# Silu made from tanh, and a causal mask added in tiles of 32 rows

## The chip, the core and the metric

The kernel runs on one core of a Trainium2 chip. The core has engines that run side by side, each through its own instructions in order: TensorE (PE: matrix products, with the weight loads shown apart as PEld), VectorE (DVE), ScalarE (ACT), GpSimd (POOL) and SyncE (SP, which here only starts transfers). They wait for each other through semaphores. PE writes to PSUM, of which this kernel uses eight banks of 128 x 512 floats. Transfers run in queues on 16 DMA engines. The metric is the device time of one execution in microseconds (us).

## The reference

The input `x` is 16 sequences of 256 rows with 128 columns. Four blocks are added to it, each after a layer normalization:

```python
x = x + attention_a(layernorm(x))      # 2 heads of 64, rotary half, softmax, full
x = x + ffn(layernorm(x))
x = x + attention_b(layernorm(x))      # 16 heads of 8, causal (see below)
x = x + ffn(layernorm(x))              # the same weights again
```

The feed-forward block has ternary weights `w` and a scale `s` for each output:

```python
h = silu(x @ w1.T * s1) * (x @ w2.T * s2)     # 128 -> 512
h = gelu(h @ h1.T * t1); h = gelu(h @ h2.T * t2)   # 512 -> 512, exact gelu
return h @ w3.T * s3                           # 512 -> 128
```

In attention b the scores are `k . q / sqrt(8)`, replaced by -10000 wherever the key's row is later than the query's, and the softmax runs over the keys.

## The kernel before, in words

**Tiles.** The 4096 rows are eight tiles (`NP`) of 512 rows, two sequences each. All of `x` stays on chip in `XR`. Each tile goes through attention a, feed-forward "f", attention b and feed-forward "g". Attention b works by sequence: for each, four groups of four heads.

**Order.** The loops at the end of `hybrid_kernel` record every operation, with the engine, an expected time and a rank, in a `Plan`. `Plan.laid` then places them in time like a list scheduler: at each step it takes, over all engines, the operation that can begin first; among those of one engine whose start is within a small margin (line 230) the one with the lowest rank wins, and `ORDER` (line 341) gives ranks by stage and tile. The planner knows that ACT needs `LOAD` more when the table of functions has to change (`mode`), and that PE loses `SWITCH` when it goes between matmuls on all 128 rows ("1"), on row tiles ("2r", "4r") and on column tiles ("2c", "4c"). Some operations are recorded with two or three engines (`either`), and the planner picks. `Plan.emit` writes the result out, so all instructions have line 291 in the profile, and groups are told apart by tile names.

**PSUM.** Four banks together are one tile `s` (`g_scores`, one slot): a group of scores fills it, and the next must wait until it is read. The other four banks are the tiles `w` (`g_bank`); every other product passes through them.

**Feed-forward** (`ffn`). For each of four parts of 128 hidden units, PE makes `pu` and `pg` in two banks. ACT computes Silu of `pu` into `u`; DVE multiplies `pg`, its scale and `u`, the gate product. Then `u` is split (`parts`) into a rounded high part and the rest, each 128 x 512, because the products with the hidden weights `h_sb` are exact only as a sum of both parts. ACT, DVE or POOL rounds; DVE or POOL subtracts. The hidden layers read all four parts; ACT computes Gelu from the bank. Three tables of ACT matter: Silu's, Gelu's and the exponential's, which both attentions need.

**Attention b.** The queries and keys of a tile are written to DRAM by SP (`far_q`, `far_k`) and read back by POOL's queue in another layout (`qk`). In the maxima step (`attention_b_max`) PE makes a group of scores with eight matmuls of 32 rows in "4r" mode: four heads lie on four groups of 32 rows, write to four banks, and run side by side. The mask is then added in the same banks by four matmuls of full height, one for each head:

```python
for a in range(4):
    o.matmul(sc[:, a, P : 3 * P], lhsT=eye[:], rhs=hide[:], start=False, stop=True, ...)
```

`eye` is the identity and `hide` a 128 x 256 table with -3e38 where a score must not count (the diagonal block, twice). DVE reduces the group to maxima, 1.75 us. Later `attention_b` makes the scores again ("4r", tiles `s`, with the maxima through `pick`), ACT takes the exponential (1.45 us), POOL cuts the upper triangle off, and PE multiplies by the values in "4c" mode.

**Set-up.** Constants are made on POOL and DVE (rank `LATER`) while the loads run. Columns of scales lie in `cols_sb`: `C_W1S` holds `s1`, `C_W2S` holds `s2`.

Of the kernel before, what the change touches and what calls it, by code (L numbers as in the profile page):

```python
# [94 lines left out]
class Plan:  # L95
# [2 lines left out]
    HOP = {"PE": 0.26, "DVE": 0.12, "ACT": 0.14, "POOL": 0.1, "SP": 0.1}  # L98
    LOAD = 1.28
    SWITCH = 0.17  # L100
    WEIGH = {"ACT": 1.54, "PE": 0.00}
    BRANCH = 1.6

    def __init__(self, nc):
# [64 lines left out]
    def laid(self):  # L169
# [28 lines left out]
        for _ in range(len(self.ops)):  # L198
            best = None
            for e, ops in ready.items():  # L200
                cands = []
                for op in ops:
                    at = max(op.at, free[e])
                    wants = {}
                    for t in op.main.tiles | op.main.claims:
                        g = t.group
                        if t.slot is None and g is not None:
                            n = wants[g] = wants.get(g, 0) + 1
                            at = max(at, sorted(g.free)[n - 1], min(t.quota.free) if t.quota else 0.0)
                    for g, n in wants.items():  # L210
                        if g.in_turn and not all(t in op.main.tiles | op.main.claims for t in g.queue[:n]):
                            at = 1e9
                    if at >= 1e8:
                        continue
                    if cut is not None and e not in behind and at >= cut:
                        at = max(at, cut + self.BRANCH)
                    cost = 0.0
                    if op.mode is not None and op.mode != mode[e]:
                        if e == "ACT" and not (isinstance(op.mode, tuple) and mode[e] in op.mode):
                            cost = self.LOAD  # L220
                        elif e == "PE" and (op.mode[0] if isinstance(op.mode, tuple) else op.mode) != mode[e]:
                            cost = self.SWITCH
                    cands.append((at, cost, op))
                if not cands:
                    continue

                weigh = self.WEIGH.get(e, 0.0)
                first = min(a + weigh * c for a, c, _ in cands)
                at, cost, op = min(
                    (x for x in cands if x[0] + weigh * x[1] <= first + 0.012),  # L230
                    key=lambda x: (order_of(x[2].main.rank), x[2].main.index),
                )
                if best is None or (at, at + cost + op.us) < (best[0], best[0] + best[1] + best[2].us):
                    best = (at, cost, op)
# [59 lines left out]
class _Recorder:  # L294
# [19 lines left out]
P = 128  # L314
# [24 lines left out]


ORDER = {
    (INPUT, "a"): (-781, 18.6),
    (MAIN, "a"): (-863, 52.3),
    (NORM, "f"): (377, 0),
    (FILL, "f"): (88, 87.2),
    (INPUT, "b"): (299, 73.8),
    (MAXIMA, "b"): (-1830, 180.0),
    (MAIN, "b"): (448, 22.6),
    (NORM, "g"): (827, 180.7),
    (FILL, "g"): (423, 113.4),  # L350
}
LATER_AT = -505


def order_of(kind):
# [20 lines left out]
def hybrid_kernel(ctx: ExitStack, tc: tile.TileContext, x, rows, cols, wa, wb, w12, h1, h2, w3, out):  # L376
# [127 lines left out]
    for t in range(2):  # L504
# [11 lines left out]
    o.tensor_scalar(rot2[:, :, 1, :], ya[:], -1.0, None, ALU.mult)  # L516
    o.tensor_scalar(rot1[:, :, 1, :], rot2[:, :, 0, :], -1.0, None, ALU.mult)


    p.rank = (LATER, "", 0, 0)  # L520
    ones = fixed([P, P], "ones")
# [2 lines left out]
    p("POOL", 0.1).memset(neg[:], NEG)  # L524


    hide = fixed([P, 2 * P], "hide", BF16)
    o = p("POOL", 0.8)
    o.memset(hide[:], 0.0)
    o.affine_select(  # L530
        out=hide[:].rearrange("p (b k) -> p b k", b=2),
        in_=hide[:].rearrange("p (b k) -> p b k", b=2),
        compare_op=ALU.is_ge,
        fill=-HUGE,
        base=0,
        pattern=[[0, 2], [-1, P]],
        channel_multiplier=1,
    )
    eye = fixed([P, P], "eye", BF16)
    p("POOL", 0.3).tensor_copy(eye[:], ident[:])  # L540

    least = fixed([P, 2], "least")
    o = p("POOL", 0.5)
# [36 lines left out]
    o.tensor_scalar(pi[:], pi[:], 31, 1, ALU.bitwise_and, ALU.arith_shift_right)  # L580
    o.tensor_tensor(pick4[:], pi[:], want[:], ALU.is_equal)
    p("DVE", 0.46).tensor_copy(pick[:], pick4[:].unsqueeze(2).to_broadcast([P, 4, P]))

    s8 = 1.0 / math.sqrt(DB)
    p("POOL", 0.3).tensor_scalar(wb_sb[:, 0:P], wb_sb[:, 0:P], s8, None, ALU.mult)
# [46 lines left out]
    def bank(name, quota=None):  # L632
        return p.tile(psum, [P, 512], F32, name, g_bank, quota)

    def sb(shape, name, g, quota=None, dtype=F32):
        return p.tile(work, shape, dtype, name, g, quota)

    def small(shape, name):

        n = math.prod(shape[1:])  # L640
# [7 lines left out]
    def layernorm_T(i, what, bias=None):  # L648
# [20 lines left out]
        for t in range(TB):  # L669
            by, mean = rstd[:, t : t + 1], mv[:, t, 0:1]  # L670
            p.either(
                ("DVE", 0.26, "tensor_scalar", (xh[:, t, :], XR[i][:, t, :], mean, by, ALU.subtract, ALU.mult), {}),
                ("ACT", 0.24, "activation", (xh[:, t, :], XR[i][:, t, :], AF.Identity), {"bias": shift[:, t : t + 1], "scale": by}),
            )
        pt = bank(f"lt_{what}{i}", ahead)
        parts = what in "fg"
# [127 lines left out]
    def attention_b_inputs(i):  # L804
# [3 lines left out]
        for name, c0, bias in (("q", 0, C_BQ), ("k", P, C_BK)):  # L808
            plus = cols_sb[:, bias : bias + 1]
            pp = bank(f"p{name}b{i}", ahead)  # L810
            hl = sb([P, 2, TOK], f"{name}hl{i}", g_16, q_hl, F32R)
            p("PE", 0.45, "1", claim=[hl]).matmul(pp[:], lhsT=wb_sb[:, c0 : c0 + P], rhs=xT[:], start=True, stop=True)
            p.either(
                ("ACT", 0.67, "activation", (hl[:, 0, :], pp[:], AF.Identity), {"bias": plus}),
                ("DVE", 0.72, "tensor_scalar", (hl[:, 0, :], pp[:], plus, None, ALU.add), {}),
            )
            p("DVE", 0.77).scalar_tensor_tensor(hl[:, 1, :], pp[:], plus, hl[:, 0, :], ALU.add, ALU.subtract)
# [24 lines left out]
    def attention_b_max(i, s, q0, k0, q1, k1, v):  # L842
# [10 lines left out]
        for g in range(4):  # L853


            sc = p.tile(psum, [P, 4, 512], F32, f"sb{n}_{g}", g_scores)
            o = p("PE", 0.28 + 0.15 + 0.42, ("4r", "1"))
            for qt, c0 in ((1, 0), (0, T)):
                for a in range(4):
                    rows = slice(32 * a, 32 * a + 32)  # L860
# [192 lines left out]
    def ffn(i, what):  # L1053
# [23 lines left out]
        for o in range(NC):  # L1077
# [11 lines left out]
        for layer, (w_sb, wv, cs) in enumerate(((h1_sb, h1v, C_H1S), (h2_sb, h2v, C_H2S))):  # L1089
# [110 lines left out]
```

## Time and profile before

| | |
|---|---|
| runs of the kernel | 787.37 us median of 3 (785.58 to 787.78) |
| profiled execution | 785.15 us; its span, first to last instruction, 783.4 us |
| busy: PE, ACT, DVE, POOL | 718.8, 529.7, 499.7, 269.5 us |
| table loads on ACT | 103, 1283 ns each |
| mask matmuls | 256 of 128 x 256 |
| Silu; gate product | 64 on ACT, 688 ns; 64 on DVE, 744 ns |
| granted PE clock, mean | 0.984 |

In the page, each engine's busy time is followed by its share of the span; the slices cut the span in 40, and a digit is the busy share in tenths. The chain goes back from the last instruction, at each step to what released it or to the instruction before it on its engine; its shares tell where the end was set. A row of a group reads: engine, operation, output tile <- input tiles, shape, count | busy us, mean ns of one | idle time ahead of them and what ended most of it. A row of waits reads: who <- for whom: us in total, times, longest. A row of a timeline reads: start, duration in us, engine, what. The end of a matmul is modelled, so starts are the better measure on PE.

### The profile page before, as it was taken

What the parts mean: (1) busy time and instruction counts of PE and PEld (TensorE: products, weight loads), DVE (VectorE), ACT (ScalarE), POOL (GpSimd) and SP (SyncE); (2) the same over time, 40 slices, a digit from 0 to 9 for tenths busy, and PEclk for the clock granted to TensorE, in tenths of its full rate; (3) what the DMA queues carried; (4) which work ended last, traced back from release to release, by engine and by line L of the source; (5) the groups of instructions that cost most, each with busy time, mean ns of one, the idle gap of its engine ahead of it and who ended that gap; (6) DMA issues with size and microseconds to landing.
All of it is one profiled execution on the core that took longest, in us unless ns stands there. A gap on an engine that the chain in (4) does not pass through costs nothing.

```text
span 783.4 us, 14329 instructions
## 1 busy us (share of the span) xinstructions
PE 718.8 (92%) x5700; PEld 510.5 (65%) x5700; DVE 499.7 (64%) x1051; ACT 529.7 (68%) x790; POOL 269.5 (34%) x422
## 2 busy tenths in 40 slices
PE   4796899988999999999999999899998989999996
PEld 2564566767677775775675768576665765756775
DVE  6887896485864866656666674856666467463641
ACT  4566777774689759776657675765768566689652
POOL 8765554042406315144325422313324233131000
PEclk9798999999999999999999999999999999999999
DMA  8400000006004225043052110404322022000000
GB/s 295 143 1 1 1 1 1 1 25 191 1 33 129 54 109 162 1 133 84 2 161 54 33 24 1 123 1 121 97 79 56 1 69 55 2 14 2 14 15 18
DMA packets 37789, 45.20 MB, mean 58 GB/s; under 512 B 1744, under 2 KB 26832, under 8 KB 37712
## 3 DMA queue, kind: packets, MB, share of 16 engines
q0 software_dynamic: 18096, 19.40, 10.2%
q1 hardware_dynamic: 19328, 24.39, 8.9%
q8 instruction: 46, 0.75, 0.4%
q10 hardware_dynamic: 288, 0.39, 0.2%
q14 instruction: 31, 0.25, 0.1%
HBM read 25.31 MB, written 18.87 MB: 56 GB/s over the span
## 4 chain that ended last, share of the span: by engine, by line
PE 64%; DVE 16%; ACT 10%; issue 4%; POOL 3%; DMA 2%; SPq 0%; POOLq 0%; DVEq 0%; ACTq 0%
PE w L291 53%; PE s L291 11%; ACT L291 3%; ACT w L291 3%; DVE u L291 2%; DVE small L291 2%; DVE h L291 2%; DVE w L291 2%; DVE m L291 2%; ACT u L291 2%; POOL w L291 1%; DVE x L291 1%; DMA x<-in_x 1%; ACT hl L291 1%; POOL rope L291 1%
## 5 line engine op out<-in xcount | busy, mean ns | idle before, releaser
L291 PE MATMUL w<-h,h_sb 128*128 128x512 f32 x1024 | 278.2, 411 | 6.2 <-DVE h L291 1.9
L291 PEld LDWEIGHTS w<-h,h_sb 128*128 128x128 f32 x1024 | 182.2, 189 | 58.2 <-issue 5.4
L291 ACT ACTIVATE u<-w,cols_sb 128x512 f32<-128x512 f32 x128 | 87.3, 687 | 76.3 <-PE w L291 75.5
L291 ACT ACT_TABLE_LOAD x103 | 132.1, 1283 | 9.5 <-DVE small L291 4.8
L291 POOL TENSOR_SCALAR_AFFINE_SELECT w<-w 128x1024 f32<-128x1024 f32 x64 | 71.7, 1120 | 192.3 <-ACT w L291 187.8
L291 DVE TENSOR_REDUCE m<-s 128x12 f32<-128x1536 f32 x64 | 112.3, 1754 | 25.2 <-PE s L291 24.6
L291 ACT ACTIVATE w<-s 128x1536 f32<-128x1536 f32 x64 | 92.9, 1451 | 25.7 <-PE s L291 20.9
L291 DVE TENSOR_TENSOR h<-u,h 128x512 fp32r<-128x512 f32 x102 | 72.7, 713 | 31.0 <-ACT h L291 28.7
L291 PE MATMUL s<-qk,qk 32*128 32x256 f32 x1024 | 73.3, 331 | 7.3 <-ACT w L291 3.6
L291 PEld LDWEIGHTS s<-qk,qk 32*128 32x128 f32 x1024 | 44.5, 184 | 47.4 <-issue 15.1
L291 DVE SCALAR_TENSOR_TENSOR u<-w,cols_sb,u 128x512 f32<-128x512 f32 x64 | 47.6, 744 | 38.6 <-ACT u L291 38.6
L291 ACT ACTIVATE hl<-w,cols_sb 128x512 f32<-128x512 f32 x64 | 41.7, 687 | 37.7 <-PE w L291 37.5
L291 PE MATMUL w<-w_sb,hl 128*128 128x128 f32 x512 | 62.1, 276 | 0.5 <-ACT hl L291 0.3
L291 PE MATMUL w<-xTffn,w_sb 128*128 128x512 f32 x128 | 57.4, 448 | 4.2 <-ACT u L291 1.8
L291 PEld LDWEIGHTS w<-w_sb,hl 128*128 128x128 f32 x512 | 59.6, 192 | 2.1 <-ACT hl L291 1.2
L291 PE MATMUL w<-w,vp 128*32 128x256 f32 (+1 forms) x1024 | 54.3, 331 | 3.6 <-POOL w L291 2.5
L291 POOL TENSOR_TENSOR h<-u,h 128x512 fp32r<-128x512 f32 x26 | 33.4, 1289 | 63.0 <-ACT h L291 51.7
L291 PE MATMUL w<-xlffn,w_sb 128*128 128x512 f32 x128 | 52.8, 413 | 1.6 <-DVE xlffn L291 1.6
L291 DVE TENSOR_TENSOR x<-w,x 128x512 f32<-128x512 f32 (+1 forms) x40 | 23.1, 579 | 47.8 <-PE w L291 47.7
L291 PEld LDWEIGHTS w<-w,vp 128*32 128x32 f32 x1024 | 27.1, 109 | 31.4 <-issue 11.1
L291 ACT CAST h<-u 128x512 fp32r<-128x512 f32 x66 | 40.9, 620 | 4.3 <-DVE u L291 2.3
L291 ACT ACTIVATE w<-s,small 128x256 f32<-128x256 f32 x64 | 29.5, 478 | 16.1 <-DVE small L291 12.7
(156 smaller groups left out, 1080.5 us busy)
## 6 DMA issues: line engine op xcount, KB each, us to landing
far_q<-w SPq DMA_DIRECT2D x16, 512.0 KB, 3.0
far_k<-w SPq DMA_DIRECT2D x16, 512.0 KB, 3.7
qk<-far_q POOLq DMA_DIRECT2D x16, 512.0 KB, 4.3
qk<-far_k POOLq DMA_DIRECT2D x16, 512.0 KB, 5.0
w<-in_h SPq DMA_DIRECT2D x2, 1024.0 KB, 11.2
h_sb<-in_h POOLq DMA_DIRECT2D x2, 1024.0 KB, 10.6
out<-x SPq DMA_DIRECT2D x8, 256.0 KB, 2.4
x<-in_x SPq DMA_DIRECT2D x7, 256.0 KB, 9.2
```

Source lines behind the costliest of these rows:

```text
L291: getattr(getattr(self.nc, self.ENGINES[op.engine]), name)(*a, **k)
```

## The change

- In `ffn`, ACT computes `tanh(s1/2 * pu)` in place of Silu; the planner may run it under the exponential's table or under Gelu's. A new DVE product makes `(u + 1) * pu` in place. The set-up halves `C_W1S` and multiplies `C_W2S` by it (two POOL instructions), so that the gate product gives the same value.
- In `attention_b_max` the mask is added by sixteen matmuls of 32 rows in place of four of 128. For each slice of 32 rows of the mask there are four, one for each head's row group, and the slice leaves out the columns ahead of it, which hold nothing: they have 256, 192, 128 and 64 columns. `eye` and `hide` become tables of four slices, 128 x 512 each, built from two iotas on POOL and five DVE instructions. The step is now all "4r".
- Expected times, ranks (`ORDER`, `LATER_AT`), the weight of a table load (`WEIGH`) and the margin in the planner have other values, so the order on every engine and the choices among engines are different.

```diff
-    WEIGH = {"ACT": 1.54, "PE": 0.00}
+    WEIGH = {"ACT": 0.37, "PE": 0.00}
...
-                    (x for x in cands if x[0] + weigh * x[1] <= first + 0.012),
+                    (x for x in cands if x[0] + weigh * x[1] <= first + 0.010),
...
-    (INPUT, "a"): (-781, 18.6),
-    (MAIN, "a"): (-863, 52.3),
-    (NORM, "f"): (377, 0),
-    (FILL, "f"): (88, 87.2),
-    (INPUT, "b"): (299, 73.8),
-    (MAXIMA, "b"): (-1830, 180.0),
-    (MAIN, "b"): (448, 22.6),
-    (NORM, "g"): (827, 180.7),
-    (FILL, "g"): (423, 113.4),
+    (INPUT, "a"): (-887, 5.0),
+    (MAIN, "a"): (-1031, 75.9),
+    (NORM, "f"): (333, 26.5),
+    (FILL, "f"): (-481, 27.8),
+    (INPUT, "b"): (371, 24.9),
+    (MAXIMA, "b"): (-1664, 7.9),
+    (MAIN, "b"): (-33, 10.3),
+    (NORM, "g"): (1277, 199.8),
+    (FILL, "g"): (-595, 156.8),
 }
-LATER_AT = -505
+LATER_AT = -277
...
+    skew = sb([P, 4, P], "skew", g_16, None, I32)
+    p("POOL", 0.7).iota(skew[:], pattern=[[-32, 4], [1, P]], base=0, channel_multiplier=0)
+    rowi = fixed([P, 1], "rowi", I32)
+    p("POOL", 0.1).iota(rowi[:], pattern=[[0, 1]], base=0, channel_multiplier=1)
+    row = fixed([P, 1], "row")
+    away = sb([P, 4, P], "away", g_16)
+    o = p("DVE", 0.7)
+    o.tensor_scalar(rowi[:], rowi[:], 31, None, ALU.bitwise_and)
+    o.tensor_copy(row[:], rowi[:])
+    o.tensor_copy(away[:], skew[:])
+    eye = fixed([P, 4, P], "eye", BF16)
+    hide = fixed([P, 4, P], "hide", BF16)
+    o = p("DVE", 0.7)
+    o.tensor_scalar(eye[:], away[:], row[:, 0:1], None, ALU.is_equal)
+    o.tensor_scalar(hide[:], away[:], row[:, 0:1], -HUGE, ALU.is_gt, ALU.mult)
...
+    p("POOL", 0.2).tensor_scalar(cols_sb[:, C_W1S : C_W1S + NC], cols_sb[:, C_W1S : C_W1S + NC], 0.5, None, ALU.mult)
+    p("POOL", 0.2).tensor_tensor(
+        cols_sb[:, C_W2S : C_W2S + NC], cols_sb[:, C_W2S : C_W2S + NC], cols_sb[:, C_W1S : C_W1S + NC], ALU.mult
+    )
...
-                ("ACT", 0.24, "activation", (xh[:, t, :], XR[i][:, t, :], AF.Identity), {"bias": shift[:, t : t + 1], "scale": by}),
+                ("ACT", 0.38, "activation", (xh[:, t, :], XR[i][:, t, :], AF.Identity), {"bias": shift[:, t : t + 1], "scale": by}),
...
-            o = p("PE", 0.28 + 0.15 + 0.42, ("4r", "1"))
+            o = p("PE", 0.55, "4r")
...
-            for a in range(4):
-                o.matmul(sc[:, a, P : 3 * P], lhsT=eye[:], rhs=hide[:], start=False, stop=True, skip_group_check=True)
+            for sl in range(4):
+                for a in range(4):
+                    rows = slice(32 * a, 32 * a + 32)
+                    o.matmul(
+                        sc[:, a, P : 3 * P].rearrange("p (b k) -> p b k", b=2)[:, :, 32 * sl : P],
+                        lhsT=eye[rows, sl, :],
+                        rhs=hide[rows, sl, 32 * sl : P].unsqueeze(1).to_broadcast([32, 2, P - 32 * sl]),
+                        start=False,
+                        stop=sl == 3,
+                        skip_group_check=True,
+                    )
...
-            p("ACT", 0.59, "silu", rank=(FIRST, what, i, 0)).activation(u[:], pu[:], AF.Silu, scale=cols_sb[:, C_W1S + o : C_W1S + o + 1])
+
+            p("ACT", 0.59, ("exp", "gelu"), rank=(FIRST, what, i, 0)).activation(
+                u[:], pu[:], AF.Tanh, scale=cols_sb[:, C_W1S + o : C_W1S + o + 1]
+            )
+            p("DVE", 0.77, rank=(FIRST, what, i, 0)).scalar_tensor_tensor(u[:], u[:], 1.0, pu[:], ALU.add, ALU.mult)
...
-                p("ACT", 0.59, "gelu", rank=(FIRST, what, i, 0)).activation(u, ph[:], AF.Gelu, scale=cols_sb[:, cs + o : cs + o + 1])
+                p("ACT", 0.65, "gelu", rank=(FIRST, what, i, 0)).activation(u, ph[:], AF.Gelu, scale=cols_sb[:, cs + o : cs + o + 1])
```

The expected times of the bias additions of attention b's inputs change too (ACT 0.67 to 0.59, DVE 0.72 to 0.66 and 0.77 to 0.67).

More of the change, by code (lines that the diff above doesn't have):

```diff
@@ L517, in hybrid_kernel, with sb @@
     o.tensor_scalar(rot1[:, :, 1, :], rot2[:, :, 0, :], -1.0, None, ALU.mult)
+    def sb(shape, name, g, quota=None, dtype=F32):
+        return p.tile(work, shape, dtype, name, g, quota)
     p.rank = (LATER, "", 0, 0)
@@ L524, in hybrid_kernel @@
     p("POOL", 0.1).memset(neg[:], NEG)
[L527 to L540, printed above, removed]
+    skew = sb([P, 4, P], "skew", g_16, None, I32)
[13 more added lines that the diff above has]
+    o.tensor_scalar(hide[:], away[:], row[:, 0:1], -HUGE, ALU.is_gt, ALU.mult)
     least = fixed([P, 2], "least")
@@ L633, in bank @@
         return p.tile(psum, [P, 512], F32, name, g_bank, quota)
-    def sb(shape, name, g, quota=None, dtype=F32):
-        return p.tile(work, shape, dtype, name, g, quota)
     def small(shape, name):
@@ L813, in attention_b_inputs @@
             p.either(
-                ("ACT", 0.67, "activation", (hl[:, 0, :], pp[:], AF.Identity), {"bias": plus}),
-                ("DVE", 0.72, "tensor_scalar", (hl[:, 0, :], pp[:], plus, None, ALU.add), {}),
+                ("ACT", 0.59, "activation", (hl[:, 0, :], pp[:], AF.Identity), {"bias": plus}),
+                ("DVE", 0.66, "tensor_scalar", (hl[:, 0, :], pp[:], plus, None, ALU.add), {}),
             )
-            p("DVE", 0.77).scalar_tensor_tensor(hl[:, 1, :], pp[:], plus, hl[:, 0, :], ALU.add, ALU.subtract)
+            p("DVE", 0.67).scalar_tensor_tensor(hl[:, 1, :], pp[:], plus, hl[:, 0, :], ALU.add, ALU.subtract)
             shape = [P, 2, 2, TOK]
```

## The prediction

> **What bounds the kernel now.** I read the page's head first (busy shares, slices), then the chain that ended last.
>
> ```profile
> span 783.4 us, 14329 instructions
> ...
> PE 718.8 (92%) x5700; PEld 510.5 (65%) x5700; DVE 499.7 (64%) x1051; ACT 529.7 (68%) x790; POOL 269.5 (34%) x422
> ...
> PE   4796899988999999999999999899998989999996
> ...
> PE 64%; DVE 16%; ACT 10%; issue 4%; POOL 3%; DMA 2%; SPq 0%; POOLq 0%; DVEq 0%; ACTq 0%
> PE w L291 53%; PE s L291 11%; ACT L291 3%; ACT w L291 3%; DVE u L291 2%; DVE small L291 2%; DVE h L291 2%; DVE w L291 2%; DVE m L291 2%; ACT u L291 2%; POOL w L291 1%; DVE x L291 1%; DMA x<-in_x 1%; ACT hl L291 1%; POOL rope L291 1%
> ```
>
> PE is busy nearly everywhere after the first tenth and holds 64% of the chain. No other engine is full, so what they cost is latency: PE waits because a result is late or a PSUM bank is not free. "ACT L291" has no tile: that is the table loads. The chain by time gives it as 3.3%, "DVE u" as 2.4%.
>
> Next come the groups by line, for the instructions that the change touches, and the sums of waits:
>
> ```profile
> L291 ACT ACT_TABLE_LOAD x103 | 132.1, 1283 | 9.5 <-DVE small L291 4.8
> ...
> L291 DVE SCALAR_TENSOR_TENSOR u<-w,cols_sb,u 128x512 f32<-128x512 f32 x64 | 47.6, 744 | 38.6 <-ACT u L291 38.6
> ```
>
> ```profile
> DVE u L291 <- ACT u L291: 38.6, 10, 8.2
> ...
> PEld w L291 <- ACT u L291: 15.5, 32, 1.5
> ...
> PEld w L291 <- DVE u L291: 8.8, 13, 1.4
> ...
> PE w L291 <- ACT u L291: 5.7, 14, 1.2
> ...
> PE w L291 <- DVE u L291: 4.3, 7, 1.2
> ```
>
> A quarter of ACT's busy time is table loads. The product after Silu waits for ACT, and PE waits 34.3 us in all on the two users of `u` and of its bank. Last, two stretches of PE's timeline, a maxima step and a score step:
>
> ```profile
> 347.90 0.51 PE L291 MATMUL s<-qk,qk 32*128 32x256 f32 x8
> 348.34 0.61 PE L291 MATMUL s<-hide,eye 128*128 128x256 bf16 x4
> 348.79 0.38 PE L291 MATMUL w<-ident,o 128*128 128x128 f32 x2
> ```
>
> ```profile
> 412.61 0.39 PE L291 MATMUL s<-qk,qk 32*128 32x256 f32 x4
> 412.83 0.29 PE L291 MATMUL s<-mT,pick 32*128 32x256 f32 x4
> 412.95 0.29 PE L291 MATMUL s<-qk,qk 32*128 32x256 f32 x4
> 413.07 0.28 PE L291 MATMUL s<-mT,pick 32*128 32x256 f32 x4
> ```
>
> In the second, four 32-row matmuls go as one round; a further round of 256 columns costs 0.12 us, the first 0.22.
>
> **The change part by part.** Counts are those of the two built programs, on the branch that runs. Times are against the profiled execution: 785.15 us, 1.75 more than its span and 2.2 below the median 787.37.
>
> *Table loads.* 103 become 58: 45 fewer, at 1.283 us 57.7 us of ACT. Low end: only those on the chain count, 3.3% of 783.4 = 25.9 us, times 45/103 = 11.3. High end: all 57.7 lie on the path. A loss is excluded, as ACT does less before the same results. I take 17, near the chain's end, for PE covers most; above it because the product waits 38.6 us for ACT, and loads push back work whose data is ready (at 413.46 a load starts right behind a Silu, and the exponential behind it starts at once at its end).
>
> *The product.* 64 DVE instructions (`u` times its bank plus bank) of the form of the 744 ns row: 47.6 us. 56 of the 64 stand directly ahead of the gate product of the same `u`, which already waited for ACT, so the wait is not new but moved one instruction up; what is queued behind it is as before (the two parts of `h`, then maxima reductions of 1754 ns). New is that the result comes one product later, and that `pu`'s bank is released by DVE, not by ACT. The planner answers by moving work: 21 subtractions of the low part go from DVE (713 ns, -15.0) to POOL (1289, +27.1), 10 fewer roundings on DVE (463, -4.6; 8 go to ACT at 620, 2 to POOL), 24 normalisations come from ACT (489) to DVE (about 450, +10.8), 11 net more evictions and bias adds of about 0.6 (+6.6). DVE grows by 45.4, to about 545 us (70%); POOL by about 29, to 38%: the hidden layers multiply the high parts first, which hides a late low part; without that cover 21 x 0.58 us = 12. Bounds: 0 if PE's other tiles cover it; all 47.6 if every product delays PE. By DVE's average (16% of 783.4 = 125 us on the chain, of 499.7 busy, so 25%) 45.4 costs 11.4; by the row "DVE u" (2.4% = 18.8 us of 47.6, 39%) the products alone cost 18.8. I take 12, nearer the average, for there is other work to run on PE in the slices where `u` is made.
>
> *ACT's other work.* 24 normalisations and about 11 evictions and bias adds leave (-11.7, -6.4), 8 roundings come (+5.0): -13, at ACT's share of the chain (78 of 530, 15%) -2. Bounds -13 and 0.
>
> *The masks.* Before, the eight score matmuls and the switch to full rows take 0.44 us to the first mask, the four masks 0.45 to the next instruction (0.37 in the trace where a hidden layer follows; I use 0.40): 0.84. After, two rounds 0.34, then four mask rounds of 256, 192, 128 and 64 columns, then the same switch (0.10) on the way out. If rounds go by columns they take 2.5 x 0.12 = 0.30, in all 0.74; if each costs a full round 0.48, in all 0.92. Over 64 groups: -6.4 to +5.1. I take -4.5: in the value products' rounds of four, 128 columns start 110 ns apart and 256 columns 215. The number of changes of row and column mode is 404 after, 407 before: no term. Weight loads rise by 768, and `PEld` waits on "issue" already; that is why I stay off the end.
>
> *Set-up and moved steps.* Masks are built by five DVE instructions and two iotas in place of three POOL instructions (1.0 us); DVE's first statistics are queued behind them, and they wait for POOL's iota, but the statistics need the first `x`, whose load is on the chain until 8.5 us (2.31 + 6.21), and three casts at 0.69 us (the row of `pick`) are done by then; without that cover about 2.5 us. Two small POOL scalings of the columns (about 0.25 each) stand before POOL's bias work and are due only at the first hidden layer. The stages' ranks move, but the 32 far copies on SP keep their order by tile (the first output stands behind the last tile's query copies, not the sixth tile's, and nobody waits for an output), and the 32 reads back on POOL begin at its 205th instruction, not the 201st. The first reads are exposed before (3.80 and 5.39 us on the chain near 176 us) and stay so: 0, bounds -5 and +5.
>
> Sum: -17 + 12 - 2 - 4.5 = -11.5, so 773.7; I say 774.
>
> *Two rules against these rows.* The start after a load follows it by 1.295 us. The Trainium skill (ScalarE: Activation LUTs, What ACT_TABLE_LOAD costs) gives a drain of about 1380 ns beside the load, 2.66 us per switch: the 45 would be worth 120 us of ACT and the first term would double; no such gap stands in ACT's timeline here. Against the change speaks the skill's TensorEngine Tiling (Array Packing), Instruction Overhead: about 60 cycles for each matmul however few its columns, and no tiling of a side that is small. Estimated from it at 2.4 GHz (TensorE: Matmul & The Clock Gate, Part 1), sixteen masks take 0.40, a group 0.84, and the term is 0 (sum 778); in this trace the four of a round start within 0.01 us of each other, so I go by rounds.
>
> **The rivals.**
>
> A, slower: the bank. `pu` has one of four banks of `w`; Silu freed it, now the product does, 0.78 us later (a product's time from start to start) and behind whatever DVE runs. Everything else is worth -17 - 4.5 - 2 = -23.5, so it decides from 30 of 64 products felt whole by PE. With 43 felt, +33.5 - 23.5 = +10: 795. For it: the 34.3 us of PE's waits on these tiles, and DVE's reductions of 1.75 us in the same queue. Against: those waits average 0.5 us, and PE has other tiles' matmuls.
>
> B, no change: loads at the chain's price (11.3), masks 0, product 11.4, -2: 783, within 0.3%. For it: each is the plain chain reading. Against: 45 loads off a 68% engine.
>
> C, larger gain: tanh runs under either table, so exponentials and gelus no longer wait to be batched; loads count half (29), the product 4: -31.5, 754. For it: single exponentials between two loads in ACT's order before. Against: PE's busy share leaves little.
>
> That the change does not do what it says is excluded for the loads by the program's count; for the masks it is the +5.1 end.
>
> **How the numbers follow.** Likeliest (a gain of 3 to 21, 764 to 782): 0.60. C: 0.14. B: 0.07. A: 0.19. The range runs from just below C to just above A, 752 to 797, with about one in ten beyond each end. About 0.3%, 2.4 us, is what a measurement of this kernel can tell from no change. Faster 0.74, same 0.07, slower 0.19.
>
> **What the profile after would show.** Loads: 58, busy near 74 us, the chain's "ACT L291" near 2%. Product: DVE near 545 us; if A holds, PE's waits on "DVE u" grow well past the 13.1 us of now. Masks: from the first mask to the next PE start about 0.4 us; if rounds are not shorter with fewer columns, 0.58. Span near 772, PE's busy share still above 90%. I would be wrong if the new order starves PE in the first 100 us, or if DVE's queue holds the score banks.

## The result: slower by 1.5%, and the profile after

The changed kernel takes 798.07 us (median of 4 runs, 795.24 to 803.14), the kernel before 786.80 (4 runs, 785.58 to 787.78). The ratio is 1.0153, with a 95% interval of 1.0121 to 1.0185. Forecast were 774 us and a gain; the sign is wrong, and the time lies just above the range (752 to 797).

The page of the changed kernel, the same parts as of before:

```profile
span 793.3 us, 15889 instructions
...
PE 714.9 (90%) x6468; PEld 515.4 (65%) x6468; DVE 554.2 (70%) x1125; ACT 459.9 (58%) x717; POOL 298.0 (38%) x446
...
PE 61%; DVE 27%; DMA 4%; ACT 4%; issue 2%; POOL 2%; DVEq 0%; POOLq 0%; ACTq 0%
...
L291 POOL TENSOR_TENSOR h<-u,h 128x512 fp32r<-128x512 f32 x47 | 60.3, 1287 | 104.5 <-ACT h L291 87.0
...
L291 ACT ACT_TABLE_LOAD x58 | 74.4, 1283 | 14.4 <-PE s L291 6.6
...
L291 DVE TENSOR_TENSOR h<-u,h 128x512 fp32r<-128x512 f32 x81 | 62.7, 774 | 20.0 <-ACT h L291 18.3
...
L291 DVE SCALAR_TENSOR_TENSOR u<-u,w 128x512 f32<-128x512 f32 x64 | 43.4, 678 | 30.9 <-ACT u L291 30.8
```

The counts are what the prediction said: 58 loads; ACT's busy time falls by 69.8 us (said: 57.7 + 13); POOL's grows by 28.5 (said: about 29); DVE's by 54.5 (said: 45.4), of which the product is 43.4. PE has 4 us less to do. And yet the span is 10 us longer. The chain tells where: ACT falls from 10% to 4%, DVE rises from 16% to 27%. The reading of this that the experiments below test: the work that left ACT was never worth its length, and what came to DVE cost more than the chain had said.

The sums of waits of the changed kernel (who <- for whom: us in total, times, longest):

```profile
DVE u L291 <- ACT u L291: 30.8, 14, 6.5
...
PEld w L291 <- DVE u L291: 23.3, 36, 1.9
...
PE w L291 <- DVE u L291: 9.6, 12, 1.6
...
PEld w L291 <- ACT u L291: 0.6, 2, 0.3
```

Before, PE waited 21.2 us for ACT's `u` and 13.1 for DVE's, 34.3 in all. Now it is 0.6 and 32.9, 33.5 in all. These sums count much of the time twice, because PE and its weight loads (PEld) often stand still together; as stretches of time they are 25.3 us before and 24.6 now. So the waits at `u` have only changed their owner; ACT's earlier results bring PE nothing there, because DVE now stands between them and PE.

Two stretches of the timeline (start, duration in us, engine, what). First PE in a maxima step, to be held against the step at 347.90 in the prediction:

```profile
331.56 0.51 PE L291 MATMUL s<-qk,qk 32*128 32x256 f32 x8
331.90 0.46 PE L291 MATMUL s<-hide,eye 32*128 32x256 bf16 x16
```

The masks begin 0.34 us after the first score matmul (0.44 before). Worked out from all 64 groups by starts: from the first score matmul to the next instruction of PE, the median is 0.808 us before and 0.732 after, about -4.9 us in all. The four mask rounds start 120, 83 and 56 ns apart, by their columns (256, 192, 128), and the four matmuls inside a round 3 to 5 ns apart (medians).

Then DVE in a stage in which `u` is made:

```profile
544.10 0.68 DVE L291 SCALAR_TENSOR_TENSOR u<-u,w 128x512 f32<-128x512 f32 x1
544.88 0.75 DVE L291 SCALAR_TENSOR_TENSOR u<-w,cols_sb,u 128x512 f32<-128x512 f32 x1
545.55 0.41 DVE L291 CAST mT<-w 128x256 fp32r<-128x256 f32 x1
545.88 0.42 DVE L291 CAST h<-u 128x512 fp32r<-128x512 f32 x1
546.33 0.69 DVE L291 TENSOR_TENSOR h<-u,h 128x512 fp32r<-128x512 f32 x1
546.94 0.68 DVE L291 SCALAR_TENSOR_TENSOR u<-u,w 128x512 f32<-128x512 f32 x1
547.72 0.75 DVE L291 SCALAR_TENSOR_TENSOR u<-w,cols_sb,u 128x512 f32<-128x512 f32 x1
548.58 0.43 DVE L291 CAST h<-u 128x512 fp32r<-128x512 f32 x1
549.04 0.69 DVE L291 TENSOR_TENSOR h<-u,h 128x512 fp32r<-128x512 f32 x1
549.65 0.68 DVE L291 SCALAR_TENSOR_TENSOR u<-u,w 128x512 f32<-128x512 f32 x1
```

DVE goes without a gap here, and one part of 128 hidden units takes it 2.7 to 2.8 us: product, gate product, rounding, subtraction, now and then a small cast. In this stretch DVE sets the pace. Taken over all 16 such stages (from the first matmul of `pu` to the last gate product), DVE is busy 76% of the time before and 84% after. The 70% of the page is an average over stages that differ.

### The profile page after: what moved, and what is told of

The parts are those of the page before. It is cut to its first block, busy times and chain, and to the rows that moved or that the text cites. A ratio compares the mean times of both kernels' runs of the same rounds, so it can differ in the third digit from the quotient of the medians.

```text
span 793.3 us, 15889 instructions
## 1 busy us (share of the span) xinstructions
PE 714.9 (90%) x6468; PEld 515.4 (65%) x6468; DVE 554.2 (70%) x1125; ACT 459.9 (58%) x717; POOL 298.0 (38%) x446
## 4 chain that ended last, share of the span: by engine, by line
PE 61%; DVE 27%; DMA 4%; ACT 4%; issue 2%; POOL 2%; DVEq 0%; POOLq 0%; ACTq 0%
PE w L291 51%; PE s L291 10%; DVE u L291 5%; DVE h L291 5%; DVE m L291 4%; DVE w L291 3%; DVE small L291 3%; ACT w L291 2%; DMA far_k<-w 2%; DMA qk<-far_k 2%; DVE xhffn L291 1%; ACT L291 1%; POOL qk L291 1%; DVE xlffn L291 1%; POOL w L291 1%
## 5 line engine op out<-in xcount | busy, mean ns | idle before, releaser
L291 PE MATMUL w<-h,h_sb 128*128 128x512 f32 x1024 | 266.9, 405 | 7.0 <-DVE u L291 3.4
L291 POOL TENSOR_TENSOR h<-u,h 128x512 fp32r<-128x512 f32 x47 | 60.3, 1287 | 104.5 <-ACT h L291 87.0
L291 DVE TENSOR_TENSOR h<-u,h 128x512 fp32r<-128x512 f32 x81 | 62.7, 774 | 20.0 <-ACT h L291 18.3
L291 PE MATMUL w<-xTffn,w_sb 128*128 128x512 f32 x128 | 59.6, 465 | 11.9 <-DVE u L291 5.6
L291 DVE SCALAR_TENSOR_TENSOR u<-u,w 128x512 f32<-128x512 f32 x64 | 43.4, 678 | 30.9 <-ACT u L291 30.8
L291 ACT CAST h<-u 128x512 fp32r<-128x512 f32 x74 | 45.9, 620 | 23.3 <-DVE u L291 21.2
L291 PE MATMUL w<-xlffn,w_sb 128*128 128x512 f32 x128 | 54.9, 429 | 0.7 <-DVE xlffn L291 0.7
```

The lines of the kernel that those rows point to most:

```text
L291: getattr(getattr(self.nc, self.ENGINES[op.engine]), name)(*a, **k)
```

## The experiments

**Theories.** *Sum*: the terms hold apart from each other, and one of them (loads, product, masks) was mis-sized. *Bank*, the mechanism of rival A: PE waits because the product frees `pu`'s bank late. *Queue*: a DVE instruction more delays all that stands behind it in DVE's order, whatever it reads. *Order*: the new order itself is better or worse.

**1. The parts, each with the order planned anew.** The first four runs combine the old and the new operations with the old and the new values of the planner (ranks, weight of a load, margin, expected times; the values are in the diff of the change).

```diff
 masks_old_order   before + masks of 32 rows              old planner values
 tanh_old_order    before + tanh and product              old planner values
 both_old_order    after's operations                     old planner values
 new_order_alone   before's operations                    new planner values
```

> The kernel before with the masks alone in 32-row tiles (planner's values of before, planned anew with the masks' own cost). Both theories: a group's step on PE goes from 0.81 to 0.73 us as in the changed kernel, 64 x 0.075 = 4.8 us less PE: about 782 beside 787. If the masks themselves were what costs (a third theory), above 790.

> The kernel before with tanh and the product alone, masks full, planner's values of before (70 table loads instead of 103). Theory DVE (the product on DVE and the bank it holds cost more than the loads give): slower than before, 793 to 800. Theory order (the planner's new values expose what was hidden, the product does not): faster, 775 to 783.

> The changed kernel with the planner's values of before (ranks, weight of a load, margin, expected times). Theory DVE: near the changed kernel, 790 to 798. Theory order: faster than before, 770 to 780.

> The kernel before, Silu and full masks, with the planner's values of the changed kernel alone. Theory order: slower, 797 to 805, with reads of attention b's inputs on the chain as in the changed kernel. Theory DVE: within 4 us of before, 783 to 791.

| run | us | ratio, 95% |
|---|---|---|
| masks_old_order | 812.75 | 1.0330 (1.0309 to 1.0350) |
| tanh_old_order | 826.47 | 1.0533 (1.0492 to 1.0573) |
| both_old_order | 828.06 | 1.0538 (1.0519 to 1.0558) |
| new_order_alone | 822.45 | 1.0462 (1.0439 to 1.0486) |

All four lose 26 to 42 us, even the masks alone, which take work from PE, and even the new values with not one operation changed. Each of the four has an order that the planner made anew from values that were set beside other operations. So this is no price of the parts, and the comparison can't separate them. It shows that the planner's values are good for one set of operations and some 27 to 36 us worse for a set that differs little. From here on every edit is made in place: the order on each engine is kept instruction by instruction, and only the instructions named are changed, left out or put in.

**2. The parts in place.** In the old order: the masks alone, tanh with its product alone, both. In the new order: the products left out.

```diff
 masks_in_place   (before)
-    o.matmul(sc[:, a, P : 3 * P], lhsT=eye[:], rhs=hide[:], ...)       # four
+    o.matmul(sc[..., 32 * sl : P], lhsT=eye4[rows, sl, :], ...)        # sixteen, as in the change
 tanh_in_place    (before)
-    act: AF.Silu
+    act: AF.Tanh, and scalar_tensor_tensor(u, u, 1.0, pu, add, mult) on DVE,
+    put in just ahead of the gate product, or of the next user of pu's bank if that comes earlier
 no_product       (after)
+    prod.calls.clear()
```

> The kernel before in its own order, instruction by instruction, with the 32-row masks put where the full ones stood (and their tables built at the head). No planning anew. Theory order (each change pays or costs little by itself, the re-planned order decides): 64 x 0.075 = 4.8 us less PE, of which PE's share of the chain, two thirds, to all is felt: 782 to 784 beside 787. If the masks cost by themselves: 790 and more.

> The kernel before in its own order, with tanh where Silu stood and each product put just ahead of its gate product, or ahead of the next use of the bank of pu where that comes first; 66 table loads, no work moved between engines. Theory DVE (the product and the bank it holds cost more than the loads give): slower than before, 790 to 800. Theory order: 37 loads fewer give as much as 64 products take, within 5 us of before, 780 to 788.

> Both in place in the order of before. Theory order: faster than the changed kernel (798) by 10 us or more, 775 to 786. Theory DVE: 787 to 797, near the changed kernel.

> The changed kernel in its own order with the 64 products left out (the gate then multiplies tanh alone, so Silu is not computed); the bank of pu is free when ACT has read it. Theory DVE: all that the product costs comes back, 772 to 780 beside 798, at 12 us and more below before. Theory order: the product is mostly hidden, 786 to 794.

| run | us | ratio, 95% |
|---|---|---|
| masks_in_place | 785.31 (12 runs) | 0.9967 (0.9944 to 0.9991) |
| tanh_in_place | 832.25 | 1.0590 (1.0567 to 1.0614) |
| both_in_place | 829.96 | 1.0562 (1.0537 to 1.0587) |
| no_product | 781.08 | 0.9933 (0.9907 to 0.9958) |

The masks are worth 2.6 us by the ratio, and 2.3 again between tanh_in_place and both_in_place: a gain, smaller than the 4.9 us that they take from PE (the end of the section on the prediction comes back to this). Without its product the changed kernel would be 4.8 us faster than the one before (785.85 in these runs). So the product costs 17 us (781.08 to 798.07), and all the rest of the change is worth 5, not the 23.5 of the prediction. The chain and the waits of no_product:

```profile
PE 58%; DVE 8%; DMA 5%; POOL 3%; issue 1%; ACT 1%; POOLq 0%; DVEq 0%; SPq 0%
```

```profile
DVE u L291 <- ACT u L291: 31.2, 14, 6.5
...
PEld w L291 <- DVE u L291: 3.3, 6, 1.1
...
PE w L291 <- DVE u L291: 0.8, 2, 0.6
```

PE's waits for DVE's `u` fall from 32.9 to 4.1 (as stretches of time, 24.0 to 3.3). The chain of this run could be followed back only to 182 us, so its shares don't add up to the span; counted from 190 us on in both runs, DVE's share of the chain falls from 22% to 11%. DVE still waits 31 us for ACT, as it does with the product, so those waits don't tell the two apart. The 16 stages in which `u` is made last 250.9 us in all before, 231.3 without the product and 256.2 with it. In the old order the same products cost far more; the waits of tanh_in_place:

```profile
PEld w L291 <- DVE u L291: 67.0, 62, 3.2
...
PE w L291 <- DVE u L291: 44.3, 49, 2.7
```

111 us, where it was 13.1 (as stretches of time, 69 and 9). That is what rival A would look like, so the bank has to be tested.

**3. Is it the bank?** The product reads `u` twice instead of `u` and the bank, so that ACT frees the bank as before (the values are then not the reference's): in the new order, and in the old one just ahead of the gate product. Or ACT copies the bank to SBUF right behind tanh, and the product reads the copy. And the loads by themselves: the old order with tanh for Silu and no product, which leaves 66 loads of 103.

```diff
 product_off_bank, in_place_off_bank
-    scalar_tensor_tensor(u[:], u[:], 1.0, pu[:], ALU.add, ALU.mult)
+    scalar_tensor_tensor(u[:], u[:], 1.0, u[:], ALU.add, ALU.mult)
 copied_by_act
+    act.calls.append(("copy", (spare, pu[:]), {}))
-    scalar_tensor_tensor(u[:], u[:], 1.0, pu[:], ALU.add, ALU.mult)
+    scalar_tensor_tensor(u[:], u[:], 1.0, spare, ALU.add, ALU.mult)
 loads_alone      (before)
-    activation(u[:], pu[:], AF.Silu, ...)
+    activation(u[:], pu[:], AF.Tanh, ...)
```

> The changed kernel in its own order with every product reading u twice in place of u and the bank of pu (so not Silu): DVE's work and its place in the queue stay, but the bank is free when ACT has read it. Theory bank (what costs is that the bank waits for DVE): most of the 17 us that came back without the product come back here too, 781 to 787 beside 798 of the changed kernel. Theory DVE time (the product's 0.68 us in a fuller queue costs): 793 to 800.

> The changed kernel in its own order, computing the same, but ACT copies the bank of pu to SBUF right behind tanh (64 copies of about 0.59 us, into one place that all share), and the product reads the copy. Theory bank: the bank is free after two ACT instructions without DVE's queue; 785 to 795, faster than the changed kernel, if the 38 us of copies stay covered on ACT, which is busy 58%. Theory DVE time: not faster, 797 to 808.

> The kernel before in its own order, tanh in place, each product just ahead of its gate product but reading u twice in place of the bank of pu (so not Silu). Theory bank: nearly all of the 46 us that tanh in place costs is gone, 780 to 795 beside 832. Theory DVE time: 815 to 832.

> The kernel before in its own order with tanh in place of Silu and no product (so not Silu): 66 table loads in place of 103, nothing added. Both theories: the gain of the loads alone; at the price of the chain's 3.3% for 37 loads 9 us, at most 48: 772 to 780.

| run | us | ratio, 95% | beside |
|---|---|---|---|
| product_off_bank | 807.52 | 1.0274 (1.0247 to 1.0302) | 798.07 with the bank |
| copied_by_act | 826.77 | 1.0516 (1.0490 to 1.0543) | 798.07 |
| in_place_off_bank | 835.12 | 1.0617 (1.0588 to 1.0647) | 832.25 with the bank |
| loads_alone | 782.09 | 0.9939 (0.9912 to 0.9966) | 786.56 before |

With the bank freed by ACT the kernel isn't faster in either order, but slower. The groups of product_off_bank and of copied_by_act show what else these edits changed, in the new order:

```profile
L291 DVE SCALAR_TENSOR_TENSOR u<-u 128x512 f32<-128x512 f32 x64 | 52.9, 826 | 31.3 <-ACT u L291 31.3
```

```profile
L291 DVE SCALAR_TENSOR_TENSOR u<-u,spare 128x512 f32<-128x512 f32 x64 | 47.8, 747 | 54.7 <-ACT spare L291 54.4
...
L291 ACT COPY spare<-w 128x512 f32<-128x512 f32 x64 | 37.5, 585 | 4.2 <-DVE u L291 4.2
```

The product without the bank takes 826 ns in place of 678: 9.5 us over 64, and the kernel lost 9.4. The copies are 37.5 us on an engine that is busy 58% of the time, and the run is 28.7 us slower; they all go to one buffer and make the product longer too (747 ns), so the 28.7 are not ACT's alone. The range of the bank theory (781 to 787) is missed by 20 us: the bank is not what the 17 us are. A few us of it aren't excluded, since the edit lengthened the product at once: PE's waits for DVE's `u` did fall, from 24.0 us to 17.2 as stretches of time. In the old one the waits of in_place_off_bank are

```profile
PEld w L291 <- DVE u L291: 38.1, 37, 3.1
...
PE w L291 <- DVE u L291: 29.2, 27, 2.9
```

67 us where it was 111, so a part of PE's waits did go with the bank, and yet the time is 2.9 us longer (the products are 734 ns here, not 679: 3.5 us). What PE doesn't wait at one place it waits at another: PE and PEld are idle together for 93.3 us of tanh_in_place and for 92.3 of in_place_off_bank.

loads_alone answers the first term. Thirty-seven loads less, 47.5 us of ACT, gave 4.5 us. Its page:

```profile
PE 64%; DVE 19%; ACT 6%; issue 4%; POOL 3%; DMA 2%; SPq 0%; POOLq 0%; DVEq 0%; ACTq 0%
...
L291 ACT ACT_TABLE_LOAD x66 | 84.7, 1283 | 8.9 <-DVE small L291 5.0
```

ACT's share of the chain falls from 10% to 6%, 32 us, and DVE's rises from 16% to 19%, 22 us. The loads alone are 1.5% of the chain where they were 3.3%: 14 us less of the chain, for 4.5 us of time. The chain is one path of many that are nearly as long: take ACT's piece off, and a path over DVE ends last instead.

**4. Latency or queue?** The product could cost because the gate product, and so `h`, comes 0.78 us later behind tanh; or because DVE's queue is 43 us longer. Four edits of the changed kernel: an instruction of the same shape in each product's place that works on a tile of its own and waits for nobody (independent_work; no product is made); the product done twice (product_twice; the second changes the values); no product, but 64 such independent instructions behind the maxima reductions, far from `u` (work_elsewhere); and the product kept, but 52 roundings of the high part moved from DVE to ACT, which relieves DVE (rounding_on_act).

```diff
 independent_work
-    scalar_tensor_tensor(u[:], u[:], 1.0, pu[:], ALU.add, ALU.mult)
+    scalar_tensor_tensor(spare[:], spare[:], 1.0, spare[:], ALU.mult, ALU.min)
 product_twice
+    prod.calls.append(prod.calls[0])
 work_elsewhere
+    prod.calls.clear()
+    red.calls.append(("scalar_tensor_tensor", (spare, spare, 1.0, spare, mult, min), {}))
 rounding_on_act
+    if op in rounds and op.engine == "DVE":
+        op.engine, op.calls = "ACT", [("copy", *op.calls[0][1:])]
```

> The changed kernel in its own order with each product replaced by a DVE instruction of the same shape that works on a place of its own and waits for nothing but DVE (so not Silu; one memset at the head makes the place). Theory DVE time in the queue: the cost stays, near the kernel with the product off the bank, whose instructions are like it (807), 800 to 810. Theory latency (what costs is that u comes one dependent step later behind tanh): most comes back, 781 to 789.

> The changed kernel in its own order with every product done twice (so not Silu). Theory that the slack is used up (the first 43 us of DVE time cost 17, the next 9.5, with the product off the bank, cost 9.4): the second 43 us cost nearly their full time, 835 to 845. Theory of a fixed share (40%): 815.

> The changed kernel in its own order without the product (781), with the 64 independent DVE instructions behind the 64 maxima reductions instead. Theory stage (DVE is the limit where u is made, 84% busy there): elsewhere the same DVE time costs less than half of what it costs there, 781 to 793. Theory tight order (a tuned order has no slack at any engine): as much as there, 800 to 810.

> The changed kernel in its own order, computing the same, with the 52 roundings of the high part that DVE does where u is made given to ACT (0.46 us each on DVE, 24 us; 0.62 on ACT, 32 us). Theory stage: DVE's time comes back there, 780 to 792. Theory tight order: ACT's added work costs more than DVE's relief gives, 800 to 820.

| run | us | ratio, 95% | price |
|---|---|---|---|
| independent_work | 799.45 | 1.0150 (1.0100 to 1.0201) | +18.4 on no_product |
| work_elsewhere | 797.52 | 1.0111 (1.0057 to 1.0165) | +16.4 on no_product |
| product_twice | 835.96 | 1.0613 (1.0572 to 1.0653) | +37.9 on the change |
| rounding_on_act | 815.63 | 1.0361 (1.0306 to 1.0415) | +17.6 on the change |

Work that nobody waits for costs what the product costs, at `u` and elsewhere. The groups of independent_work:

```profile
L291 DVE SCALAR_TENSOR_TENSOR spare<-spare 128x512 f32<-128x512 f32 x64 | 53.4, 834 | 0.0
```

So DVE's time in its queue alone is enough for a price like the product's, and it is not special to the stages in which `u` is made. The step behind tanh isn't free, though. product_off_bank has nearly the same DVE time at the same place (52.9 us, here 53.4) and also leaves the bank to ACT; all that it has more is that the product waits for tanh and the gate product for it, and it is 8 us slower than independent_work (807.52 and 799.45, each good to some 4). How the 17 us of the real product divide between queue, step and bank isn't shown. The price is not linear either. The first 43 us cost 17, the next 44 cost 38, though the second product also puts one more step behind tanh; the busy shares of product_twice give no hint of it:

```profile
PE 734.1 (88%) x6468; PEld 523.1 (63%) x6468; DVE 595.8 (71%) x1189; ACT 460.9 (55%) x717; POOL 297.6 (36%) x446
```

And it is not DVE alone: the roundings took 27 us from DVE and put 32 on ACT, and the kernel lost 17.6 us. ACT takes its work in order, and a rounding needs DVE's `u`: ahead of its roundings ACT stands idle for 55.9 us until DVE has made `u`, where it was 21.2.

**5. The two orders crossed.** Before's work in the order of the change, in place (Silu, full masks, no product; 120 loads, since this order changes tables more often with Silu in it); and in the old order, loads_alone with the 64 independent instructions behind the maxima reductions.

```diff
 old_work_new_order   (after)
-    activation(u[:], pu[:], AF.Tanh, ...)
+    activation(u[:], pu[:], AF.Silu, ...)      # and prod.calls.clear(), full masks
 old_order_elsewhere  (loads_alone)
+    red.calls.append(("scalar_tensor_tensor", (spare, spare, 1.0, spare, mult, min), {}))
```

> The order of the changed kernel, instruction by instruction, with the operations of before in it: Silu (so 120 table loads, not 58), no product, full masks. Theory tight order (an order carries the work it was planned for; more than that is felt, most of it): of the 62 added loads (80 us of ACT) half or more is felt on top of the 781 without the product and some 3 for the masks: 820 to 850. If the new order is the better one and ACT's 58% is room: 785 to 800.

> The kernel before in its own order with tanh and no product (so not Silu; 782) and the 64 independent DVE instructions behind the 64 maxima reductions. Theory tight order: about as much as the products cost at u in this order (50), 815 to 835. Theory stage (only the stages of u have no room on DVE): 785 to 800.

old_work_new_order took 837.50 us, 1.0649 (1.0583 to 1.0714); old_order_elsewhere 806.16, 1.0249 (1.0202 to 1.0296). The page of the first:

```profile
PE 63%; ACT 16%; DVE 11%; DMA 4%; issue 3%; POOL 2%; ACTq 0%; POOLq 0%; DVEq 0%
...
L291 ACT ACT_TABLE_LOAD x120 | 154.0, 1283 | 16.3 <-PE s L291 6.6
```

Against no_product, 62 loads more (79.5 us of ACT) and the full masks cost 56.4 us, and ACT is 16% of the chain. In the old order, taking 37 loads away gave 4.5. A load has no price of its own: in the order that was made with it, it was nearly free, and where it comes on top, it is felt by more than half.

In the old order the 64 instructions behind the maxima cost 24.1 us, between what the two theories expected; the products at `u` cost 50.2 and 53.0. So there a product at `u` is twice as dear. Whether the place does that or the wait for tanh isn't shown, as the old order has no run with independent work at `u`.

## Why the prediction was wrong, point by point

What each piece of added or removed engine time was felt by, from the runs above (differences of medians, good to one to six us by the intervals; the medians of the kernel before in the five groups of runs lie between 785.7 and 786.6):

| edit | engine time | felt | share |
|---|---|---|---|
| 37 loads less, old order | ACT -47.5 | -4.5 | 0.1 |
| product, new order | DVE +43.4 | +17.0 | 0.4 |
| independent work behind the maxima, new order | DVE +49.6 | +16.4 | 0.3 |
| second product, new order | DVE +44.0 | +37.9 | 0.9 |
| copies, new order | ACT +37.5, DVE +4.4 | +28.7 | 0.7 |
| 62 loads and full masks, new order | ACT +79.5, PE +4.9 | +56.4 | 0.7 |
| independent work behind the maxima, old order | DVE +49.6 | +24.1 | 0.5 |
| product, old order | DVE +43.1 | +50.2 | 1.2 |

- **The loads: "I take 17, near the chain's end", with a low end of 11.3.** This step failed, and it is the largest part of the miss. The count (45) was right. The price came from the chain's share, taken for a lower bound: a load on the chain would be worth its length. loads_alone measured 4.5 us for 37, that is 0.12 us each, about half of what the chain's share gives for 37 (9.3). A share of the chain is no lower bound on what a removal gives, since another path ends last as soon as the piece is gone; here it was DVE's. All of the change but its product is worth 5 us, where the prediction had 23.5 for loads, masks and ACT's other work. How these 5 divide in the new order wasn't measured; the old order has 4.5 for the loads and 2.6 for the masks.
- **The product: "I take 12, nearer the average".** It cost 17 us, well inside the bounds of 0 and 47.6, and near the second reading that the prediction had (18.8, by the row "DVE u"). The duration was overrated (678 ns, not 744), the share underrated: 0.4 of its time was felt, not a quarter. The stages in which `u` is made, where DVE was 76% busy, don't explain that, since independent work behind the maxima cost 16.4 us; an average share of the chain was too low a price wherever the work stood. That the wait behind tanh would not be new was right in the main (DVE waits 30.8 us for ACT there, 38.6 before), and independent_work shows that the queue alone can cost as much. New, the prediction said, is that the result comes one product later; product_off_bank against independent_work, 8 us, says that this step is felt too.
- **"The masks: -4.5".** PE's time fell by 4.9 us, near what was worked out from the columns of the rounds; felt were 2.6. Here the Trainium skill (TensorEngine Tiling (Array Packing), Instruction Overhead) was weighed against the row: about 60 cycles for each matmul however few its columns, so no gain. The trace decides for the rows: the sixteen start in four rounds, 3 to 5 ns apart inside one, and the rounds shorten with their columns.
- **The rule on loads.** The same for the Trainium skill's drain of about 1380 ns beside each load (ScalarE: Activation LUTs, What ACT_TABLE_LOAD costs): no such gap is in ACT's rows (the next instruction starts 1.295 us after the load's start, median, before and after), and the runs put a removed load at 0.12 us, not at 2.66.
- **The planner's moves.** 47 subtractions on POOL and 81 on DVE came as said. DVE's mean for one rose from 713 to 774 ns, which the prediction didn't have (see below); with longer roundings (518 ns for 463) that is 8 us of DVE's growth beyond what was said.
- **Rival A, 795 us.** Its time is the nearest to the result, and its sign and its pattern (PE's waits on "DVE u" well past 13.1, at 32.9) came true. Its mechanism is not what costs: with the bank freed by ACT the kernel is slower still, so that its time is near the result is luck. As stretches of time, PE waits for DVE's `u` 3.3 us in no_product, 11.0 in independent_work, 17.2 in product_off_bank and 24.0 in the changed kernel, whose times are 781.1, 799.5, 807.5 and 798.1. So the queue, the step behind tanh and perhaps the bank each add waits there, but these waits don't measure the price.
- **Transfers.** DMA's share of the chain rose from 2% to 4%, which could pass for a cause. no_product has 5% (38 us, the changed kernel 34) and is faster than the kernel before, so it isn't.
- **Rival C** had one thing right: tanh runs under either table without a load. That freedom brought the loads down to 58. Without its product, all that was worth 5 us.
- **The two signs of being wrong that it named.** PE is busy for 72.2 of the first 100 us, 73.6 before: the new order doesn't starve it there. DVE's queue does hold the score banks longer (the row "PEld s" on "DVE m" goes from 10.4 to 19.0 us), but no_product has 16.6 there and is faster, so this isn't the main loss.

What stays open: which waits add up to the 17 us one by one; why the old order takes twice as much for a product at `u` as for work behind the maxima; how much of the loss goes with the clock (last section); and whether another search of the planner's values would find an order in which tanh wins. The room for that is bounded by these runs only for the orders that they had: without its product, the changed kernel is 5 us faster than before, so a product that is hidden whole would leave 5.

The fastest complete kernel of all these is masks_in_place, the kernel before with the masks in tiles of 32 rows and nothing else: 785.31 us, 0.33% below before by the ratio, with an interval of 0.09% to 0.56%. Its runs fall in two groups, four from 780.1 to 780.9 and eight from 783.7 to 787.5, so the median shows less of it than the ratio. The four were granted a clock of 0.985 and the eight 0.977 to 0.981; four runs of the kernel before at 0.985 took 785.2 to 787.0. At the same clock, then, the masks are worth about what they take from PE.

## What to carry to other kernels

In a program whose order was searched for its own operations, a removed piece and an added piece of the same length have different prices: here the removed ones gave a tenth of their time, and the added ones took a third to all of it, on engines that were busy 58 to 70%. So cost a trade of ACT time for DVE time with the gain near zero and the price at a third of its time or more until a run has measured it, and take the chain's share of an engine as a hint, not as a bound from either side. When waits are added up, don't add PE's and PEld's for the same tile: they are largely the same time. And test a part in place: planning anew with values that go with other operations moved the time by 27 us here for masks that are worth -2.6 by themselves.

## What the runs showed of the hardware that was not expected

**Some of DVE's two-input products take far longer when both inputs lie in SBUF, and POOL is busy then.** The same 128 x 512 float product takes 652 to 689 ns with the second input in PSUM, never more (64 times in the changed kernel). With both in SBUF the median is nearly the same, 684 ns (680), but 15 of 64 in product_off_bank take over a tenth longer, up to 1880, and the mean is 826. During the long ones POOL is busy for 82% of their time, during the others for 17%; in independent_work it is 78% and 20%. In the changed kernel's products POOL is busy for 35% of the time, and none is long. The Trainium skill (SBUF — State Buffer, SBUF: two separate sides) has a pair of ports that an operation with two SBUF inputs and a GpSimd operation (one that reads SBUF) take in turn, each holding it to its end; the rows agree with that, though no run here stopped POOL to show it. It made product_off_bank a worse test of the bank than it was meant to be, since the change freed the bank and lengthened the product at once; its 9.4 us are about that length, and what the freed bank gave can't be told apart from it. It would also explain why DVE's subtractions, whose inputs are both in SBUF, went from 713 to 774 ns when POOL had more to do; that was not tested.

**The granted PE clock differs between executions, and the time with it.** The runs of the kernel before were granted 0.976 to 0.992, and took 790.4 us at the lowest and 783.0 at the highest, about 5 us for each 0.01. The changed kernel's four runs go the same way (795.2 at 0.977, 803.1 at 0.965). Its mean is 0.971, the kernel before has 0.983; by the slope of the runs before, an estimate, about 6 of its 11 us go with the clock. Whether the clock makes the time longer, or more waiting of PE brings a lower clock, isn't shown. It is no account of the product's price: no_product, with a mean of 0.973, is 17 us faster than the changed kernel at nearly the same clock. Nor does the clock order different kernels: new_order_alone takes 822 us at 0.971.
